# Moved fills, a fold among the first maxima, and layer 1's shift through a small transpose: a two-layer transformer kernel

## The chip, the cores and the metric

The kernel runs on one core of a Trainium2 chip. The metric is device time in microseconds of one launch. The kernel before took 1236.22 us (median of three runs, 1233.09 to 1239.17). One more execution was taken under the profiler; its rows are the durations quoted here.

## The reference, cut to what matters

Two transformer layers over 2048 tokens of 128 channels, all in float32. Each layer is: modulation (a 128-vector through a sigmoid-linear unit and a 128x768 matrix gives six vectors: shift, scale and gate, twice), a layer norm, attention, a gated residual, a second norm, a feed-forward part and a gated residual.

```python
mod = (_silu(L0_c) @ L0_wmod).reshape(...)      # sa, ca, ga, sb, cb, gb
ga = (2 * (ga >= 0) - 1) * jnp.maximum(jnp.abs(ga), 0.25)     # gb alike
h = _layernorm(x) * (1 + ca) + sa
x = x + ga * _L0_attn_ref(h, ...)   # 16 heads of 8, softmax over all 2048 keys
h = _layernorm(x) * (1 + cb) + sb
x = x + gb * _L0_ffn_ref(h, ...)    # 16 experts, one per token, and a shared one
...
x = x + ga * _L1_attn_ref(h, ...)   # 8 query heads of 16, one key head, causal
x = x + gb * _L1_ffn_ref(h, ...)    # mixes each token with the one before it
```

## The kernel before, in words

**Engines.** A planner takes the program as written and gives each engine its own order: an instruction is placed when the planner thinks its inputs ready, the earliest written first. `tc.keep_in_program_order(ins)` pins an instruction behind the one written before it on its engine. On the chip each engine then runs its list strictly in that order.

**Start.** `first_norm` takes the four blocks of 512 tokens: statistics on DVE, square root (L648) on ACT, reciprocal and normal on DVE, four transposes on PE, and the eviction into `hT` on ACT (L237). `modulation(0)` runs between.

**Stacks.** A product of two float32 numbers is made from two reduced-precision halves each, hi and lo. Keys and queries are split (`split`, L239), and their halves are stacked in four interleaved row sets by DMAs (`stack`, L256), so that one pass over 64 rows per head gives the whole product. Layer 0 has 8 stacks (`kS0`), two heads each. Every eighth row set ends in a row of ones for the shift: `fill(st)` (L669) writes a whole stack [128 x 2048] from `last_rows`, a column with ones at rows 31, 63, 95 and 127, before the DMAs write the other rows. Fills 0 and 1 are written ahead of `first_norm`; fills 2 to 7 in `begin0`, each ahead of its stack's DMAs. All eight are on ACT. Stacks 0 and 1 go out on SP and ACT, the others on SP alone.

**Attention** (L287) runs units (block b of 512 queries, group of four heads): 16 units in layer 0 and 8 in layer 1. `first_pass(u)` makes the scores [128 queries x 1024] and takes their maxima on DVE (L385, or L390 with the causal mask). `largest` (L394) negates them and splits each into two halves in `nm`. `turn` (L411) transposes `nm` so that the negated maxima, called the shift, become rows. `second_pass(u)` makes the scores the other way round (L458), exponentiates them on ACT (L468) and multiplies them with the values on PE (L484). The first pass runs eight steps (`LEAD`) ahead of the second. Three score banks in PSUM are shared by both passes; two more serve the values and everything else (`other_bank`).

In layer 0 (`fused`) the turn is one transpose of 32 columns, a copy and eight DMAs on SP (L424), which put the rows into the query stack. In layer 1 `nm` is [128 x 4 x 128] with the maxima at the first columns of each 64; four transposes give `mT` with the rows in place, and two extra products (L464) add them. A turn is called two or three steps after its unit's last maximum (`turns`, L438 and L591). `turn` is written after `project_q(b + 1)` in layer 1 for the units with the first group of a block: `project_q` (L348) is put into `ready` while unit 2b's first pass runs, and ends in 16 DMAs on SP into a query stack that two blocks share.

**Fold.** `fold0` (L810) makes layer 1's modulation and gates, spreads a gate over the weights of the shared expert (GpSimd, L815) and folds the first gate into the output weights of attention. It is the first of the `late` pieces, which are taken during unit 0's second pass.

Of the kernel before, what the change touches and what calls it, by code (L numbers as in the profile page):

```python
# [10 lines left out]
F32 = mybir.dt.float32  # L11
# [8 lines left out]
P = 128  # L20
T = 2048
# [22 lines left out]
def two_layers(ctx: ExitStack, tc: tile.TileContext, a: dict, out: bass.AP):  # L44
# [48 lines left out]

    last_rows = const.tile([P, 1], F32, name="last_rows")
    nc.vector.tensor_reduce(last_rows, ident[:, 31::32], AX.X, ALU.add)


    mods = []  # L100
    sg = const.tile([P, 2], F32, name="sg")
    sc = const.tile([P, 2], F32, name="sc")

    def modulation(layer, ps):
        if layer == 0:
            nc.scalar.activation(sg, vcol(V_C0, 2), AF.Sigmoid)
            nc.vector.tensor_mul(sc, sg, vcol(V_C0, 2))
        for j in range(6):
            nc.tensor.matmul(ps[:, j:j + 1], wmod[layer][:, j * P:(j + 1) * P],
                             sc[:, layer:layer + 1], start=True, stop=True)  # L110
# [25 lines left out]
    for i, at in enumerate((ident.rearrange("p (r c) -> p r c", c=4)[:, :, 2:4],  # L136
# [24 lines left out]
    nc.gpsimd.affine_select(out=ones_f, in_=ones_f, compare_op=ALU.is_gt, fill=0.0,  # L161
                            base=0, pattern=[[1, P]], channel_multiplier=-1)
    before_r = const.tile([P, P], F32R, name="before_r")
    nc.scalar.copy(before_r, ones_f)

    rank = const.tile([P, NE], F32, name="rank")
    for e in range(NE):
# [119 lines left out]
    def attention(layer, hT, ngrp, dk, scale, causal, kvp, begin, prepare, wq, bq, folded, ended,  # L287
# [23 lines left out]
        with ExitStack() as s:  # L311
# [26 lines left out]
            negmax = []  # L338
            for i in range(2):
                shape = [P, nst, TB, S, 2] if fused else [P, TB, P]  # L340
                t = kvp.tile(shape, F32, name=f"{L}nm{i}", tag=f"nm{i}")
                nc.gpsimd.memset(t, 0.0)
                negmax.append(t)

            units = [(b, grp) for b in range(NB) for grp in range(ngrp)]
            attended = {}
# [1 line left out]
            def project_q(b):  # L348
                if b in qS:
                    return  # L350
                ps = other_bank()
                nc.tensor.matmul(ps, wq, hT[:, b * QB:(b + 1) * QB], start=True, stop=True)
# [13 lines left out]
                qS[b] = t  # L366

            def first_pass(u):
# [5 lines left out]
                def step(i, kb, pair):  # L374
                    own = causal and kb == b
                    n = (i + 1) * P if own else QB
                    ps = ps_s.tile([P, 2, QB], F32, name=f"{L}p1_{u}_{i}_{kb}_{pair}", tag="s")
                    for j in range(2):
                        g = 2 * pair + j
                        st, r = grp * nst + g // S, RT * (g % S)  # L380
                        nc.tensor.matmul(ps[:, j, :n], qS[b][r:r + RT, st, i * P:(i + 1) * P],  # L381
                                         kS(st)[r:r + RT, kb * QB:kb * QB + n],
                                         start=True, stop=True)
                    if not own:
                        nc.vector.tensor_reduce(pm[:, i, 2 * pair:2 * pair + 2, kb], ps,  # L385
                                                AX.X, ALU.max)
                    for j in range(2 if own else 0):

                        g = 2 * pair + j
                        nc.vector.tensor_tensor_reduce(  # L390
                            masked[:, :n], ps[:, j, :n], later[:, QB - n:], 1.0, LOWEST,
                            ALU.add, ALU.max, pm[:, i, g, kb:kb + 1])

                def largest():  # L394
# [3 lines left out]
                    if fused:  # L398


                        parts = [(nm[:, k],
                                  nx[:, :, k * S:(k + 1) * S]) for k in range(nst)]
                    else:

                        parts = [(nm.rearrange("p t (g w) -> p t g w", w=RT)[:, :, :, 2 * k:],
                                  nx[:, :, k * S:(k + 1) * S]) for k in range(nst)]
                    for v, nk in parts:
                        nc.vector.tensor_copy(v[:, :, :, 0].bitcast(F32R), nk)
# [2 lines left out]
                def turn():  # L411
                    nm = negmax[u % 2]
                    ps = other_bank()
                    if fused:
                        n = nst * TB * 2 * S
                        mT = qp.tile([n, P], F32R, name=f"{L}mT{u}", tag="mT")
                        nc.tensor.transpose(ps[:n, :P], nm.rearrange("p k t g w -> p (k t g w)"),  # L417
                                            ident)
                        nc.scalar.copy(mT, ps[:n, :P])  # L419

                        for k in reversed(range(nst)):
                            for i in range(TB):
                                r = (k * TB + i) * 2 * S
                                nc.sync.dma_start(  # L424
                                    out=qS[b][31::32, grp * nst + k,
                                              i * P:(i + 1) * P].bitcast(F32),
                                    in_=mT[r:r + 2 * S, :].bitcast(F32))
                    else:
                        mT = qp.tile([P, QB], F32R, name=f"{L}mT{u}", tag="mT")
                        for i in range(TB):  # L430
                            nc.tensor.transpose(ps[:, i * P:(i + 1) * P], nm[:, i, :], ident)
                        nc.scalar.copy(mT, ps)
                    shift[u] = mT

                steps = [(lambda i=i, kb=kb, pair=pair: step(i, kb, pair))
                         for i in range(TB) for kb in range(nkb) for pair in range(HG // 2)]
                last = steps.pop()
                return steps + [lambda: (last(), largest(), turns.append([0, turn]))]  # L438

            def second_pass(u):  # L440

# [114 lines left out]


            shift, late, turns, weights, ready = {}, [], [], [], []
            if not folded:
                late.append(lambda: folded.extend(fold0(other_bank())))  # L560

            def all_first():
                for u in range(len(units)):
# [3 lines left out]
                    for i, step in enumerate(first_pass(u)):  # L567
# [66 lines left out]
    def first_norm():  # L634

        with tc.tile_pool(name="ln0", bufs=2) as wp, \
# [3 lines left out]
            def start(b):  # L640
# [25 lines left out]
    pool = a0.enter_context(tc.tile_pool(name="a0kv", bufs=1))  # L666
    kS0 = pool.tile([P, H0 * RT // P, T], F32R, name="kS0", tag="kS")

    def fill(st):  # L669

        nc.scalar.activation(kS0[:, st, :], last_rows.to_broadcast([P, T]), AF.Copy)

    for st in range(2):
        fill(st)
# [3 lines left out]
    def begin0(ep, pp, stacks):  # L678
# [14 lines left out]
        for pair in range(NB // 2):  # L693
# [5 lines left out]
            cols = slice(pair * 2 * QB, (pair + 1) * 2 * QB)  # L699
            split(ps.rearrange("p j n -> p (j n)"), vcol(V_BK), hi[:, cols], lo[:, cols])  # L700

        for st in range(nst):
            rows = slice(st * 2 * D0, (st + 1) * 2 * D0)
            queues = (nc.sync, nc.scalar) if st < 2 else (nc.sync,)
            if st >= 2:
                fill(st)
            stack(kS[:, st, :], (hi[rows], lo[rows]), (0, 1, 0, 1), queues, RT // D0)
            stack(stacks[0][:, st, :], (qhi[rows], qlo[rows]), (0, 0, 1, 1), queues, RT // D0)
        for b in range(NB):
            for pair in range(TB // 2):  # L710
                ps = pp.tile([P, 2, QB], F32, name=f"pv{b}{pair}", tag="s")
                for j in range(2):
# [94 lines left out]

    gb = const.tile([P, P], F32, name="gb")

    def fold0(bank):  # L810
        modulation(1, bank)
        gates(1)
        nc.tensor.matmul(bank[:, :P], m[:, 5:6].to_broadcast([P, P]), ident, start=True, stop=True)
        nc.scalar.copy(gb, bank[:, :P])
        nc.gpsimd.tensor_tensor(wsd, wsd, gb.unsqueeze(1).to_broadcast([P, NS, P]), ALU.mult)  # L815
        wog, rows = fold_gate(pool, bank, wo0, vcol(V_BO), m[:, 2:3], "a0")
        for b in range(NB):
            add_rows(b, rows)
        return [wog]

    folded1 = []

# [546 lines left out]
```

## Time and profile before

The profiled execution took 1246.91 us, of which the span from the first to the last instruction is 1245.2 us. The mean granted clock of the tensor engine was 0.942.

| engine | busy us | share of the span | instructions |
|---|---|---|---|
| PE (matmul) | 1146.1 | 92% | 9216 |
| PEld (weight load) | 519.8 | 42% | 9216 |
| DVE | 953.1 | 77% | 1550 |
| ACT | 766.6 | 62% | 845 |
| POOL | 85.0 | 7% | 152 |

How to read it: a share of busy time is a mean over the whole span. The parts that the change touches lie in the first 100 us (start and unit 0) and in the stretch from 920 to 1220 us (layer 1's attention), so they have to be looked at there. "SPq" and "ACTq" are the queues of the two engines that issue DMAs; an issue of about half a microsecond occupies the queue, and the landing comes later. In rows of the timeline, the first number is the start from the span's beginning, the second the length, and a bracket at the end tells how long the engine had been idle and what released it.

### The profile page before, as it was taken

What the parts mean: (1) busy time and instruction counts of PE and PEld (TensorE: products, weight loads), DVE (VectorE), ACT (ScalarE), POOL (GpSimd) and SP (SyncE); (2) the same over time, 40 slices, a digit from 0 to 9 for tenths busy, and PEclk for the clock granted to TensorE, in tenths of its full rate; (3) what the DMA queues carried; (4) which work ended last, traced back from release to release, by engine and by line L of the source; (5) the groups of instructions that cost most, each with busy time, mean ns of one, the idle gap of its engine ahead of it and who ended that gap; (6) DMA issues with size and microseconds to landing.
All of it is one profiled execution on the core that took longest, in us unless ns stands there. A gap on an engine that the chain in (4) does not pass through costs nothing.

```text
span 1245.2 us, 22565 instructions
## 1 busy us (share of the span) xinstructions
PE 1146.1 (92%) x9216; PEld 519.8 (42%) x9216; DVE 953.1 (77%) x1550; ACT 766.6 (62%) x845; POOL 85.0 (7%) x152
## 2 busy tenths in 40 slices
PE   4579999999999999999999999979858999999995
PEld 2233333334433443343343343447624444444443
DVE  4788898899889889889989883343458688898532
ACT  6107777777777777777777778643323355556763
POOL 2002000000000000000000000320321011100101
PEclk9658999999999999999999999999967789999997
DMA  4841010212220212110000000033210101000000
GB/s 125 113 50 35 2 51 3 70 28 77 70 70 2 69 39 79 56 53 2 1 2 2 2 2 2 20 118 91 64 30 15 35 1 35 1 1 1 2 22 13
DMA packets 63880, 45.23 MB, mean 36 GB/s; under 512 B 7009, under 2 KB 57825, under 8 KB 63265
## 3 DMA queue, kind: packets, MB, share of 16 engines
q1 hardware_dynamic: 61008, 40.37, 13.2%
q10 hardware_dynamic: 1744, 1.32, 0.6%
q0 software_dynamic: 1024, 2.10, 0.6%
q8 instruction: 73, 1.20, 0.4%
q14 instruction: 31, 0.25, 0.1%
HBM read 9.88 MB, written 21.95 MB: 26 GB/s over the span
## 4 chain that ended last, share of the span: by engine, by line
PE 80%; DVE 12%; ACT 4%; DMA 1%; issue 1%; another core or an unknown queue 1%; DVEq 0%; SPq 0%; ACTq 0%; POOLq 0%; POOL 0%
PE a0bank L484 24%; PE a0p L458 17%; PE a0p L381 13%; PE a1bank L484 5%; PE a1p L458 4%; DVE a0mx L385 3%; DVE a1mx L385 3%; PE a1p L381 2%; PE a1p L464 2%; DVE a1masked L390 2%; PE sg L987 2%; ACT a0e L468 1%; PE gu L1039 1%; PE a0bank L522 1%
## 5 line engine op out<-in xcount | busy, mean ns | idle before, releaser
L385 DVE TENSOR_REDUCE a0mx<-a0p 128x2 f32<-128x1024 f32 x512 | 623.9, 1225 | 71.3 <-PE a0p L381 61.4
L468 ACT ACTIVATE a0e<-a0p 128x1024 f32<-128x1024 f32 x512 | 521.8, 1024 | 178.7 <-PE a0p L458 154.1
L484 PE MATMUL a0bank<-a0e,vA 128*32 128x256 f32 x4096 | 333.2, 391 | 1.7 <-ACT a0e L468 1.7
L381 PE MATMUL a0p<-kS,a0qS 64*128 64x512 f32 x1024 | 248.2, 480 | 26.4 <-DVE a0mx L385 13.1
L458 PE MATMUL a0p<-a0qS,kS 64*128 64x512 f32 x1024 | 260.5, 497 | 0.0
L468 ACT ACTIVATE a1e<-a1p 128x1024 f32<-128x1024 f32 (+3 forms) x160 | 143.1, 896 | 109.8 <-PE a1p L464 106.6
L458 PEld LDWEIGHTS a0p<-a0qS,kS 64*128 64x128 f32 x1024 | 97.2, 184 | 204.4 <-issue 132.2
L381 PEld LDWEIGHTS a0p<-kS,a0qS 64*128 64x128 f32 x1024 | 100.2, 192 | 111.4 <-ACT a0e L468 57.1
L484 PEld LDWEIGHTS a0bank<-a0e,vA 128*32 128x32 f32 x4096 | 86.3, 108 | 137.8 <-issue 121.5
L385 DVE TENSOR_REDUCE a1mx<-a1p 128x2 f32<-128x1024 f32 x96 | 115.8, 1221 | 14.5 <-PE a1p L381 13.7
L484 PE MATMUL a1bank<-a1e,vA 128*32 128x256 f32 (+1 forms) x1152 | 97.1, 386 | 0.4 <-POOL a1e L471 0.4
L458 PE MATMUL a1p<-a1qS,kS 64*128 64x512 f32 (+3 forms) x320 | 77.7, 470 | 5.2 <-DVE a1mx L385 3.9
L381 PE MATMUL a1p<-kS,a1qS 64*128 64x512 f32 (+3 forms) x320 | 68.2, 426 | 11.4 <-DVE a1mx L390 5.1
L390 DVE CUSTOM_DVE_ANT_0 a1masked<-a1p,later 128x128 f32<-128x128 f32 (+3 forms) x128 | 62.4, 488 | 10.6 <-PE a1p L381 5.2
L793 POOL DMA_INDIRECT sent<-hs,row_i x16 | 16.0, 999 | 707.6 <-DVE ln11xn L229 684.0
L464 PE MATMUL a1p<-a1mT,a1ones 64*128 64x512 f32 (+3 forms) x320 | 62.5, 379 | 0.0
L458 PEld LDWEIGHTS a1p<-a1qS,kS 64*128 64x128 f32 x320 | 32.0, 191 | 63.8 <-issue 25.5
L381 PEld LDWEIGHTS a1p<-kS,a1qS 64*128 64x128 f32 x320 | 33.1, 201 | 38.5 <-DVE a1mx L390 12.7
L484 PEld LDWEIGHTS a1bank<-a1e,vA 128*32 128x32 f32 x1152 | 25.7, 109 | 42.6 <-issue 35.3
L471 POOL TENSOR_SCALAR_AFFINE_SELECT a1e<-a1e 128x256 f32<-128x256 f32 x64 | 26.0, 407 | 234.7 <-ACT a1e L468 234.7
L464 PEld LDWEIGHTS a1p<-a1mT,a1ones 64*128 64x128 f32 x320 | 32.5, 195 | 1.7 <-issue 1.3
L419 ACT CAST a0mT<-a0bank 32x128 fp32r<-32x128 f32 x16 | 4.0, 253 | 41.2 <-PE a0bank L417 41.2
(384 smaller groups left out, 698.7 us busy)
## 6 DMA issues: line engine op xcount, KB each, us to landing
sent<-blank SPq DMA_DIRECT2D x68, 256.0 KB
kS<-a0qS SPq DMA_DIRECT2D x28, 128.0 KB
a0qS<-a0mT SPq DMA_DIRECT2D x128, 2.0 KB
wgu_sb<-in_gate_up SPq DMA_DIRECT2D x1, 2048.0 KB
a0qS<-a0qh SPq DMA_DIRECT2D x62, 32.0 KB
a0qS<-a0ql SPq DMA_DIRECT2D x62, 32.0 KB
xs<-sent SPq DMA_DIRECT2D x31, 64.0 KB
y_rows<-y SPq DMA_DIRECT2D x7, 256.0 KB
```

Source lines behind the costliest of these rows:

```text
L381: nc.tensor.matmul(ps[:, j, :n], qS[b][r:r + RT, st, i * P:(i + 1) * P], kS(st)[r:r + RT, kb * QB:kb * QB + n], start=True, stop=True)
L385: nc.vector.tensor_reduce(pm[:, i, 2 * pair:2 * pair + 2, kb], ps, AX.X, ALU.max)
L390: nc.vector.tensor_tensor_reduce(masked[:, :n], ps[:, j, :n], later[:, QB - n:], 1.0, LOWEST, ALU.add, ALU.max, pm[:, i, g, kb:kb + 1])
L458: nc.tensor.matmul(ps[:, j, q0:], kS(st)[r:r + RT, kt * P:(kt + 1) * P], qS[b][r:r + RT, st, q0:], start=True, stop=fused)
L464: nc.tensor.matmul(ps[:, j, q0:], ones[r:r + RT, g // S, :], shift[u][r:r + RT, q0:], start=False, stop=True)
L468: nc.scalar.activation(e[:, :, q0:], ps[:, :, q0:], AF.Exp, scale=scale)
L471: nc.gpsimd.affine_select(out=e[:, :, q0:q0 + P], in_=e[:, :, q0:q0 + P], compare_op=ALU.is_ge, fill=0.0, base=0, pattern=[[0, 2], [1, P]] ...
L484: nc.tensor.matmul(av[g * W:(g + 1) * W, c0:c1], vA(kt, grp * HG + g), held[kt, g // 2][:, g % 2, c0:c1], start=(kt == 0 and c0 == 0), sto ...
L522: nc.tensor.transpose(ps[:, i * P:(i + 1) * P], o[:, i * P:(i + 1) * P], ident)
L793: nc.gpsimd.indirect_dma_start(out=sent[t], in_=hs[:, i, :], in_offset=None, out_offset=bass.IndirectOffsetOnAxis(ap=row_i.bitcast(U32)[:, ...
L987: nc.tensor.matmul(ps[:, j, :], w[:, k * P:(k + 1) * P], hT[:, b * QB:(b + 1) * QB], start=True, stop=True)
L1039: nc.tensor.matmul(ps[:, i, :], xsT[q][:, i * P:(i + 1) * P], wgu[:, bass.ds(regs[j], 1), :].rearrange("p a f -> p (a f)"), start=True, st ...
```

## The change

In the start, `last_rows` gets a second column. The first is now summed on GpSimd, and the first square root is pinned behind fills 0 and 1 on ACT. Fills 2 to 7 are made by GpSimd from the second column, which DVE copies, pinned behind the last split of the keys. A second tile, `before_f`, takes the masked ones, so that `ones_f` is not written over. A small exp at the end of `begin0` loads its table there.

In unit 0's first pass, `fold0` becomes three pieces that are taken after steps 5, 11 and 17, with the modulation's products pinned. The maxima of the first eight steps of unit 1 are pinned, so is `project_q(1)`'s product, and the turn of unit 0 is called two steps sooner.

In layer 1 unit 0 keeps the four transposes (of a tile `wide`). Units 1 to 7 take one transpose of 32 columns, a copy, and eight DMAs on SP into `rows_of`, two tiles whose other rows are zero.

```diff
-    last_rows = const.tile([P, 1], F32, name="last_rows")
-    nc.vector.tensor_reduce(last_rows, ident[:, 31::32], AX.X, ALU.add)
+    last_rows = const.tile([P, 2], F32, name="last_rows")
+    first = last_rows[:, 0:1]
+    nc.gpsimd.tensor_tensor(first, ident[:, 31:32], ident[:, 63:64], ALU.add)
+    for i in (95, 127):
+        nc.gpsimd.tensor_tensor(first, first, ident[:, i:i + 1], ALU.add)
...
+                rows_of = [kvp.tile([P, QB], F32R, name=f"{L}rows{i}") for i in range(2)]
+                nc.gpsimd.memset(rows_of[1].bitcast(F32), 0.0)
...
+                if fused and b == 1:
+                    tc.keep_in_program_order(product)
...
+                        if fused and u == 1 and i == 0:
+                            tc.keep_in_program_order(found)
...
-                    if fused:
-                        n = nst * TB * 2 * S
-                        mT = qp.tile([n, P], F32R, name=f"{L}mT{u}", tag="mT")
...
+                    n = nst * TB * 2 * S
+                    if fused or u:
+                        small = qp.tile([n, P], F32R, name=f"{L}mT{u}", tag="mT")
+                        nc.tensor.transpose(
+                            ps[:n, :P], nm.rearrange("p a t b w -> p (a t b w)"), ident)
+                        nc.scalar.copy(small, ps[:n, :P])
+                        for c in reversed(range(nst if fused else S)):
                             for i in range(TB):
...
+                                if fused:
+                                    dst = qS[b][31::32, grp * nst + c, cols]
+                                else:
+                                    dst = rows_of[u % 2][c * RT:c * RT + 4, cols]
+                                nc.sync.dma_start(out=dst.bitcast(F32),
+                                                  in_=small[r:r + 4, :].bitcast(F32))
...
-                return steps + [lambda: (last(), largest(), turns.append([0, turn]))]
+                return steps + [lambda: (last(), largest(),
+                                         turns.append([2 if fused and u == 0 else 0, turn]))]
...
-            if not folded:
-                late.append(lambda: folded.extend(fold0(other_bank())))
+            folds = [] if folded else fold0(other_bank, folded)
...
                         step()
+                        if folds and i % 6 == 5:
+                            folds.pop(0)()
...
-                nc.scalar.activation(rstd, mv[:, :, 1], AF.Sqrt, bias=eps)
+                root = nc.scalar.activation(rstd, mv[:, :, 1], AF.Sqrt, bias=eps)
+                if b == 0:
+                    tc.keep_in_program_order(root)
...
-    def fill(st):
-
-        nc.scalar.activation(kS0[:, st, :], last_rows.to_broadcast([P, T]), AF.Copy)
+    def fill(st, i=0):
+
+        dst, src = kS0[:, st, :], last_rows[:, i:i + 1].to_broadcast([P, T])
+        if i == 0:
+            nc.scalar.activation(dst, src, AF.Copy)
+        else:
+            nc.gpsimd.tensor_copy(dst, src)
...
+        tc.keep_in_program_order(nc.vector.tensor_copy(last_rows[:, 1:2], last_rows[:, 0:1]))
+        for st in range(2, nst):
+            fill(st, 1)
...
-            if st >= 2:
-                fill(st)
...
+        t = lnp.tile([P, TB], F32, name="exptable", tag="y")
+        nc.scalar.activation(t[:, :1], vA[:, NT - 1, :1], AF.Exp, scale=0.0)
...
+    def fold0(bank, folded):
+        def second():
+            modulation(1, bank(), tc.keep_in_program_order)
+            gates(1)
+        def first():
+            ps = bank()
...
+        def fold():
+            wog, rows = fold_gate(pool, bank(), wo0, vcol(V_BO), m[:, 2:3], "a0")
+            for b in range(NB):
+                add_rows(b, rows)
+            folded.append(wog)
+        return [second, first, fold]
```

More of the change, by code (lines that the diff above doesn't have):

```diff
@@ L102, in two_layers, with modulation @@
     sc = const.tile([P, 2], F32, name="sc")
-    def modulation(layer, ps):
+    def modulation(layer, ps, place=lambda ins: ins):
         if layer == 0:
@@ L108, in modulation @@
         for j in range(6):
-            nc.tensor.matmul(ps[:, j:j + 1], wmod[layer][:, j * P:(j + 1) * P],
-                             sc[:, layer:layer + 1], start=True, stop=True)
+            place(nc.tensor.matmul(ps[:, j:j + 1], wmod[layer][:, j * P:(j + 1) * P],
+                                   sc[:, layer:layer + 1], start=True, stop=True))
         m = const.tile([P, 6], F32, name=f"mod{layer}", tag=f"mod{layer}")
@@ L160, in two_layers @@
     nc.scalar.copy(ones_r, ones_f)
-    nc.gpsimd.affine_select(out=ones_f, in_=ones_f, compare_op=ALU.is_gt, fill=0.0,
+    before_f = const.tile([P, P], F32, name="before_f")
+    nc.gpsimd.affine_select(out=before_f, in_=ones_f, compare_op=ALU.is_gt, fill=0.0,
                             base=0, pattern=[[1, P]], channel_multiplier=-1)
     before_r = const.tile([P, P], F32R, name="before_r")
-    nc.scalar.copy(before_r, ones_f)
+    nc.scalar.copy(before_r, before_f)
     rank = const.tile([P, NE], F32, name="rank")
@@ L337, in attention @@
             masked = kvp.tile([P, QB], F32, name=L + "masked") if causal else None
[L338 to L343, printed above, removed]
+            negmax = [kvp.tile([P, nst, TB, S, 2] if fused else [P, S, TB, nst, 2], F32,
+                               name=f"{L}nm{i}", tag=f"nm{i}") for i in range(2)]
+            if not fused:
+                wide = kvp.tile([P, TB, P], F32, name=L + "wide")
+                nc.gpsimd.memset(wide, 0.0)
+                rows_of = [kvp.tile([P, QB], F32R, name=f"{L}rows{i}") for i in range(2)]
+                nc.gpsimd.memset(rows_of[1].bitcast(F32), 0.0)
             units = [(b, grp) for b in range(NB) for grp in range(ngrp)]
@@ L351, in project_q @@
                 ps = other_bank()
-                nc.tensor.matmul(ps, wq, hT[:, b * QB:(b + 1) * QB], start=True, stop=True)
+                product = nc.tensor.matmul(ps, wq, hT[:, b * QB:(b + 1) * QB], start=True,
+                                           stop=True)
+                if fused and b == 1:
+                    tc.keep_in_program_order(product)
                 hi = kvp.tile([P, QB], F32R, name=f"{L}qh{b}", tag="qh")
@@ L384, in step @@
                     if not own:
-                        nc.vector.tensor_reduce(pm[:, i, 2 * pair:2 * pair + 2, kb], ps,
-                                                AX.X, ALU.max)
+                        found = nc.vector.tensor_reduce(pm[:, i, 2 * pair:2 * pair + 2, kb], ps,
+                                                        AX.X, ALU.max)
+                        if fused and u == 1 and i == 0:
+                            tc.keep_in_program_order(found)
                     for j in range(2 if own else 0):
@@ L402, in largest @@
                                   nx[:, :, k * S:(k + 1) * S]) for k in range(nst)]
+                    elif u:
+                        parts = [(nm[:, :, :, k].rearrange("p g t w -> p t g w"),
+                                  nx[:, :, k * S:(k + 1) * S]) for k in range(nst)]
                     else:
-                        parts = [(nm.rearrange("p t (g w) -> p t g w", w=RT)[:, :, :, 2 * k:],
+                        parts = [(wide.rearrange("p t (g w) -> p t g w", w=RT)[:, :, :, 2 * k:],
                                   nx[:, :, k * S:(k + 1) * S]) for k in range(nst)]
@@ L413, in turn @@
                     ps = other_bank()
-                    if fused:
-                        n = nst * TB * 2 * S
-                        mT = qp.tile([n, P], F32R, name=f"{L}mT{u}", tag="mT")
[L417 to L421, printed above, removed]
-                            for i in range(TB):
[L423 to L427, printed above, removed]
+                    n = nst * TB * 2 * S
[5 more added lines that the diff above has]
+                        for c in reversed(range(nst if fused else S)):
+                            for i in range(TB):
+                                cols = slice(i * P, (i + 1) * P)
+                                r = (c * TB + i) * 4
+                                if fused:
[4 more added lines that the diff above has]
+                                                  in_=small[r:r + 4, :].bitcast(F32))
                     else:
-                        mT = qp.tile([P, QB], F32R, name=f"{L}mT{u}", tag="mT")
                         for i in range(TB):
-                            nc.tensor.transpose(ps[:, i * P:(i + 1) * P], nm[:, i, :], ident)
-                        nc.scalar.copy(mT, ps)
+                            nc.tensor.transpose(ps[:, i * P:(i + 1) * P], wide[:, i, :], ident)
+                        nc.scalar.copy(rows_of[0], ps)
+                    mT = None if fused else rows_of[u % 2]
                     shift[u] = mT
@@ L808, in two_layers @@
     gb = const.tile([P, P], F32, name="gb")
[L810 to L819, printed above, removed]
+    def fold0(bank, folded):
[4 more added lines that the diff above has]
+            ps = bank()
+            nc.tensor.matmul(ps[:, :P], m[:, 5:6].to_broadcast([P, P]), ident, start=True,
+                             stop=True)
+            nc.scalar.copy(gb, ps[:, :P])
+            nc.gpsimd.tensor_tensor(wsd, wsd, gb.unsqueeze(1).to_broadcast([P, NS, P]), ALU.mult)
+        def fold():
[4 more added lines that the diff above has]
+        return [second, first, fold]
     folded1 = []
```

## The prediction

> **What bounds the kernel now.** I read the page's slices first, then the chain of waits over the first 160 us, then tables by stretch, then the timeline at the places that the change touches.
>
> The slices (31 us each):
>
> ```profile
> PE   4579999999999999999999999979858999999995
> DVE  4788898899889889889989883343458688898532
> PEclk9658999999999999999999999999967789999997
> ```
>
> From slice 4 to slice 26 PE is full at nearly the whole clock: layer 0's attention is bound by PE. Slices 0 to 3 are not, and that is where the first half of the change works. Layer 1 (from slice 29) is bound by PE again, with DVE close behind: from 1020 to 1070 us PE is busy 47.8 of 50 us and DVE 44.8.
>
> The chain of waits at the start (start, length, what):
>
> ```profile
> 19.36 1.80 ACT kS L671
> 21.16 0.67 ACT hT L237
> 21.82 1.80 ACT kS L671
> 23.62 0.67 ACT hT L237
> ...
> 39.43 3.75 DMA kS<-a0qS
> 43.18 0.79 PE a0p L381 x2
> 44.00 36.30 DVE a0mx L385 x32
> ```
>
> Three things in it: fills of kS (L671) alternate with the hT evictions on ACT; then the stacking DMAs hold everything until 43.1; then DVE's 32 maxima of unit 0 run back to back. The table by stretch (length, then busy PE, PEld, DVE, ACT, POOL with counts, clock, DMA share, GB/s) shows what limits each:
>
> ```profile
> 44.00:80.20 36.20, 25.44 (x66) 9.00 (x64) 36.20 (x32) 0.00 (x0) 0.00 (x0) 0.50 0.80 92
> 80.20:98.20 18.00, 12.74 (x41) 7.51 (x41) 13.00 (x31) 5.34 (x8) 5.77 (x5) 0.50 0.00 1
> ```
>
> In the first DVE has no gap, 36.20/32 = 1.13 us a step, while PE has 0.34 us idle a step. In the second nobody is full: 18 us in which DVE does 10 maxima (11.3 us) and waits 5. The timeline there:
>
> ```profile
> 84.32 4.59 SPq L424 DMA_DIRECT2D a0qS<-a0mT  x8
> 84.65 2.72 PE L109 MATMUL a0bank<-sc,wmod_sb 128*128 128x1 f32 x12
> 88.14 2.36 DVE L385 TENSOR_REDUCE a0mx<-a0p 128x2 f32<-128x1024 f32 x2 [1.76 <-PE a0p L381]
> 92.92 0.79 PE L458 MATMUL a0p<-a0qS,kS 64*128 64x512 f32 x2
> ```
>
> PE does layer 1's modulation just where unit 0's second pass should start, and DVE runs dry.
>
> **Part A, fills and roots (0 to 43 us).** Fills 0 and 1 ran at 13.55 to 17.45 on ACT because last_rows came from DVE at 13.47. With three GpSimd adds after ident (ready at 1.82) they fit from 3.57, when ACT has issued its DMAs. ACT then has two fills of 1.90, two table loads of 1.28 and the sigmoid's 0.20 before the first root: 3.57 + 6.56 = 10.1, against 8.17 before. Its reader, the reciprocal, ran at 11.89, behind DVE's wait for the modulation, so this is free; if Copy needs a table load of its own it is 11.4, still free. The evictions then follow their transposes. DVE's own order sets them: its work between 10.9 and 16.1 stays, then two reciprocals and two normals (2 x 1.25) bring the last xn to about 18.6, and hT3 to 19.8 instead of 24.29: 4.5 us earlier. Project_q(1)'s product (1.92 us of PE at 20.07) leaves this place too. Next, the split of pk waited for the fill at 26.55 to 28.45, some 1.0 us, which goes: the last lo ends at about 26.9 instead of 32.27. Gain at this point 5.4.
>
> The fills of stacks 2 to 7 go to GpSimd behind that lo. No row has one of 128x2048. Nearest: the cast of 128x256 at 0.394, eight times 3.15; by the slope of the 128x4096 memset (3.50) 1.9. I take 2.0: six fills from 27 to 39 (to 46 at the dear end). They are read by DMAs for units 1 to 3, and unit 1's maxima start near 73: hidden. GpSimd beside DVE: the maxima during L285's adds (93.7 to 98.6) took 1.22 to 1.28 as elsewhere, so I count nothing.
>
> The landing that PE waited for at 43.0 was a 32 KB piece of ql issued on ACT at 37.22, stuck behind the 128 KB pieces of stacks 0 and 1 and of later stacks that SP had put into the same engines. Stacks 0 and 1 are 8 x 128 KB and 16 x 32 KB, about 1.3 MB to the last piece. Between 30 and 46 the DMAs moved 131 GB/s. If later stacks do not mix in (they wait for a fill until 29 at least), the last lands near 34.5, a gain of 8.6; if they do as now, the gain is the 5.4 above. I take 7.0.
>
> **Part B, fold and turn (43 to 98 us).** Among unit 0's maxima the fold costs DVE its small operations: some 16 at 0.07 and the 0.29 of wog, 1.3. Its 12 pinned products hold PE 2.7 us. DVE has at most two filled banks, 2.3 us, and PE needs 0.79 for the next: about 1.2 lost. Two or four products of 0.2 to 0.3 later fit into the slack. A DVE wait for the products at the low clock, as at 10.91 (2.35), could add 2. Sum 2.5 to 4.5; I take 3.
>
> After unit 0 the maxima of unit 1 are pinned behind the negated maxima, so nm is ready 0.6 after the 32nd maximum, not 2.8 (L409 ended at 82.98). Eight DMAs of 2 KB: SP is 4.59 us issuing them, first packets 1.2 after the first issue, last at 89.5, 5.3 after the cast. The shift lands about 0.6 + 0.7 + 5.3 = 6.6 after the 32nd maximum; the eight steps ahead need 9.0. The score gets its bank after the sixth (7.3), and exp follows at 8.7. Before it was 95.52 - 80.21 = 15.3. Gain 15.3 - 8.7 - 3 = 3.6. Exp's table load (94.22, 1.28) is inside this. The Trainium skill (ScalarE: Activation LUTs, "What ACT_TABLE_LOAD costs") prices a switch at 2.66 with its drain; here exp started at 95.52, right behind the 1.28, so the row decides; by the page B would gain 1.4 more. Project_q(1)'s product now lies in PE-bound work: minus 1.0. **B gains 2.6**, between 0.5 and 5.
>
> **Part C, layer 1's shift.** Units 1 to 7 save PE three of four transposes: four take 0.66 in the chain, one 0.26 (L417): 7 x 0.39 = 2.7, and PE is the bound. ACT's cast falls from 0.58 to 0.25. But the rows then go through eight DMAs on SP. The rows of unit 4 (the cast, the first product that reads it, and the DMAs of project_q(3)):
>
> ```profile
> 1044.74 0.58 ACT L432 CAST a1mT<-a1bank 128x512 fp32r<-128x512 f32 x1 [2.18 <-PE a1bank L431]
> 1045.76 1.11 SPq L260 DMA_DIRECT2D a1qS<-a1qh  x2
> 1046.70 0.39 PE L464 MATMUL a1p<-a1mT,a1ones 64*128 64x512 f32 x2
> ```
>
> From the start of the cast to its first reader there are 1.96 us here. In units 1 to 7, by the same rows: 3.96, 6.62, 11.29, 1.96, 7.75, 3.30, 5.65. The new way needs, from the old start of the cast, -0.3 (fewer transposes) + 0.25 + 5.3 + 0.1 = 5.4. Late: unit 1 by 1.4, unit 4 by 3.4, unit 6 by 2.1; 6.9 in all. PE is in order, so L381 for the next maxima stands behind the waiting L464, and DVE lives on two banks, 2.3 us. The skill (DMA: Bandwidth & Descriptors, "Anatomy of one DMA") gives a small DMA a fixed cost of about 2.0 us, mostly the receipt: by it only unit 4 is late, by 0.1, and C is a gain of 2.6. This trace shows eight issues of 0.57 in line, so the row decides. How much of 6.9 is covered is unknown: nothing (the wait sits in PE's queue) to all of it (products of the first pass and of L484 placed ahead of the score). I take half, 3.5. **C costs 0.8**, between -2.7 and +4.2.
>
> **Sum.** -7.0 - 2.6 + 0.8 = -8.8 against the profiled execution (1246.91; span 1245.2 and 1.7 around it), about 1238. It ran 10.7 above the median of the runs, 1236.22; I take the same difference off that: **1227.5**. Bounds: -8.6 - 5 - 2.7 = 1220; -5.4 - 0.5 + 4.2 = 1234.5.
>
> **Rivals.**
> 1. The shift's wait is not covered at all: 6.9 instead of 3.5, so 1231. For it: DVE is nearly full at unit 4, so a dry DVE is lost. Against: L484 and L381 stand near each boundary and could be put first.
> 2. SP's order, the slower side. Project_q(b+1) is written before the turn of unit 2b, and its 16 DMAs wait in SP's queue for the last scores of the block that owned the buffer:
>
> ```profile
> SPq L260 <- PE a1p L458: 97.7, 2, 51.1
> ```
>
> If they stand ahead of the turn's eight at unit 4, these start at 1056 (16 at 0.65 from 1045.76), land at 1061, 14.8 late instead of 3.4; with 2 covered that is 11 more: 1239. If at unit 2 as well (issues from 983.6 to 994.6, needed at 985.9, 14 late): 1251. It decides as soon as the 16 come first. For it: at unit 4 the cast ends only 0.8 before those DMAs are free. Against: at unit 2 that margin is 4 us.
> 3. The front gains less: the DMAs land as late as now after the split, and DVE waits for the fold: -5.4 - 0.5 + 0.8, so 1231.
>
> **Chances.** Forecast 0.57, rival 1 0.13, rival 2 0.18, rival 3 0.12. The range for eight in ten is 1220 to 1239: it takes in the bounds and the one-boundary case of rival 2. Half a per cent, about what a measurement here can tell from no change, is 6.2 us, so faster means below 1230. The forecast gives most of it, the rivals 1 and 3 mostly "same", rival 2 slower in two of three: faster 0.52, same 0.30, slower 0.18.
>
> **What would show it.** Right: the last hT eviction near 20; the second score product near 36 instead of 43.1; the first exp near 85 instead of 95.5; L464's wait for a DMA at units 1, 4 and 6, each under 3.5 us. Wrong: a start of the maxima after 40; a DVE gap over 3 us at the modulation; any L464 that waits over 5 us, with project_q's DMAs ahead of the turn's on SP.

## The result, and the profile after

The changed kernel took 1244.94 us (median of nine runs, 1242.19 to 1252.92), against 1238.63 us of the kernel before on the same chip (nine runs, 1233.09 to 1240.67). The ratio of the means is 1.0072, interval 1.0046 to 1.0098: slower by 0.7%, some 9 us (6.3 between the medians). In a later session, on another chip, the same two kernels gave 1257.75 and 1246.45 us, ratio 1.0087 (1.0074 to 1.0100). The forecast was 1227.5.

The profiled execution of the changed kernel took 1244.0 us (span 1241.2), 3 us less than that of the kernel before. This comparison misleads. The chain of waits of the kernel before has this piece, in the experts' stage, which the change doesn't touch:

```profile
900.84 9.88 another core or an unknown queue
```

PE, DVE and ACT all stand still for 6.9 us of it. The same stop, of 9.67 to 9.89 us, is in every profile of the two sessions in which the kernel before took 1246 to 1247 us. It is in no profile of a changed or tried kernel from the sessions in which the kernel before took 1236 to 1239 us, the first profile of the changed kernel among them. Its cause is not known, but it is of the size by which the profile before, which has it, ran above its runs (10.7 us). So the profiles have to be read stage by stage, and totals compared only within one session.

The slices of the changed kernel, as before 31 us each:

```profile
PE   5669999999999999999999999979878996999995
DVE  5798898889889889889899982353487896897532
PEclk9559999999999999999999999999976997998997
```

Slices 0 to 2 are still not full (slice 3 was nearly full before, too, though the prediction counts it with them). The start, in the timeline of PE (start, length, engine, line, operands, count, and in brackets how long PE was idle and for what):

```profile
20.73 2.07 PE L713 MATMUL pq<-hT,wq_sb 128*128 128x512 f32 x2 [0.87 <-ACT hT L241]
22.60 4.50 PE L721 MATMUL pk<-hT,wk_sb 128*128 128x512 f32 x8
...
35.95 0.80 PE L390 MATMUL a0p<-kS,a0qS 64*128 64x512 f32 x2 [3.60 <-DMA kS<-a0qS]
39.31 1.65 PE L390 MATMUL a0p<-kS,a0qS 64*128 64x512 f32 x6 [2.57 <-DMA kS<-a0qS]
```

The last hT eviction ends at 20.68, near the 19.8 forecast. But pq takes 2.07 us for the two products that took 1.12 before, pk 4.50 for 3.60. In two stretches, counting only what writes or reads pk (length, then busy PE, PEld, DVE, ACT with counts, clock, DMA share, GB/s), a step shows:

```profile
22.60:24.30 1.70, 1.70 (x2) 0.67 (x2) 0.00 (x0) 0.00 (x0) 1.00 0.00 0
24.79:26.94 2.15, 2.15 (x6) 0.76 (x4) 0.37 (x1) 1.11 (x1) 1.00 0.44 90
```

The first two products fill 1.70 us; the last five fill 2.15 (the sixth in the count is the end of the one before), half the time each, 0.43 us. The clock column is no help here: the profile has no record of the clock ahead of the step to full speed at 24.41 us, and 1.00 is printed in its absence. In the kernel before that record begins at 22.58, ahead of pq, so that pq and pk ran fast there from the first product.

The second score product starts at 39.31. The chain tells what it waited for:

```profile
32.64 6.47 DMA kS<-a0qS
39.12 0.20 issue
39.31 0.81 PE a0p L390 x2
40.15 2.37 DVE a0mx L394 x2
```

The second maximum, from which DVE runs almost without gaps, starts at 40.15 instead of 44.00: 3.85 us earlier. (In the second profile of the same kernel, experiment 3, it starts at 42.44; the step of the clock came at 28.11 there. So places in the start vary by some 2 us from one profile to the next.) Then by stretch (length, busy PE, PEld, DVE, ACT, POOL with counts, clock, DMA share, GB/s):

```profile
42.40:78.20 35.80, 27.16 (x78) 12.64 (x78) 35.07 (x48) 0.53 (x2) 8.86 (x6) 0.50 0.77 87
78.20:88.50 10.30, 5.96 (x17) 2.14 (x17) 10.28 (x13) 1.28 (x2) 0.86 (x1) 0.50 0.01 2
88.50:100.00 11.50, 11.50 (x66) 4.14 (x67) 7.60 (x7) 6.45 (x7) 0.00 (x0) 0.67 0.04 9
```

DVE has no gap in the second stretch any more, where it had 5 us; in the third PE is full, but at two thirds of its clock. The first exp starts at 87.05 instead of 95.52, 8.5 us earlier, but the eleventh at 105.14 instead of 109.68, and the last of layer 0 at 806.43 instead of 812.57: the front is worth 4 to 6 us of the 9.6 forecast. The granted clock goes from 0.50 to 1.00 at 96.1 us here and at 101.1 in the kernel before, so only 5 us of the exps' lead were kept by the clock.

Layer 1 gives more than that back. SP's queue at unit 4, then PE:

```profile
1024.57 2.59 SPq L442 DMA_DIRECT2D a1rows<-a1mT  x4
1027.26 1.14 SPq L264 DMA_DIRECT2D a1qS<-a1qh  x2
...
1036.08 1.23 SPq L264 DMA_DIRECT2D a1qS<-a1ql  x2
1037.36 2.52 SPq L442 DMA_DIRECT2D a1rows<-a1mT  x4
```

```profile
1032.37 0.94 PE L560 MATMUL a1bank<-a1wog,a1onT 128*128 128x128 f32 x6
1041.05 1.85 PE L481 MATMUL a1p<-a1rows,a1ones 64*128 64x512 f32 x6 [7.75 <-DMA a1rows<-a1mT]
```

Four of the turn's eight DMAs (L442) stand ahead of project_q(3)'s 16 (L264), the other four behind them. The shift's product starts 16.8 us after the cast (1024.29), and PE stands for 7.75 us. At units 1, 6 and 7 it waits for the same DMAs by 1.58, 1.71 and 1.10 us.

### The profile page after: what moved, and what is told of

Its sections match the earlier page's. It is cut to its first block, busy times and chain, and to the rows that moved or that the text cites. A ratio compares the mean times of both kernels' runs of the same rounds, so it can differ in the third digit from the quotient of the medians.

```text
span 1241.2 us, 22639 instructions
## 1 busy us (share of the span) xinstructions
PE 1149.3 (93%) x9195; PEld 520.0 (42%) x9195; DVE 955.8 (77%) x1550; ACT 754.7 (61%) x840; POOL 96.3 (8%) x159
## 4 chain that ended last, share of the span: by engine, by line
PE 81%; DVE 10%; ACT 3%; DMA 2%; SPq 1%; issue 1%; ACTq 0%; DVEq 0%; POOL 0%; POOLq 0%
PE a0bank L501 24%; PE a0p L475 18%; PE a0p L390 13%; PE a1bank L501 5%; PE a1p L475 4%; DVE a0mx L394 3%; PE a1p L390 3%; PE a1p L481 3%; PE sg L1024 2%; DVE a1masked L401 2%; DVE a1mx L394 1%; ACT a0e L485 1%; PE gu L1076 1%; ACT a1e L485 1%; PE a0bank L539 1%
## 5 line engine op out<-in xcount | busy, mean ns | idle before, releaser
L390 PEld LDWEIGHTS a0p<-kS,a0qS 64*128 64x128 f32 x1024 | 100.2, 192 | 106.9 <-ACT a0e L485 58.0
L390 PE MATMUL a1p<-kS,a1qS 64*128 64x512 f32 (+3 forms) x320 | 72.2, 434 | 8.9 <-DVE a1mx L401 4.5
L481 PE MATMUL a1p<-a1rows,a1ones 64*128 64x512 f32 (+3 forms) x320 | 65.5, 396 | 12.1 <-DMA a1rows<-a1mT 12.1
L481 PEld LDWEIGHTS a1p<-a1rows,a1ones 64*128 64x128 f32 x320 | 34.8, 203 | 14.7 <-issue 14.2
L998 ACT ACTIVATE sigs<-sg 128x512 f32<-128x512 f32 x12 | 7.2, 598 | 24.8 <-PE sg L1024 24.8
```

Of the source, the lines that this page charges most:

```text
L481: nc.tensor.matmul(ps[:, j, q0:], ones[r:r + RT, g // S, :], shift[u][r:r + RT, q0:], start=False, stop=True)
```

## The experiments

Ratios are to the kernel before, measured in the same session. There were four: experiments 1 to 4; 6 to 8; 5 with the repeats marked "again"; and 9. Places in a profile are compared across sessions only where the text says so, and differences there of less than some 2 us decide nothing.

**1. The front alone.** Layer 1's turn is the old one, with its layout of `nm`; the line that decides:

```diff
-                    if fused or u:
+                    if fused:
```

> The changed kernel with layer 1's old shift (four transposes of 128 columns, no DMA), so parts A and B alone. In the changed kernel's profile unit 0's second maximum came 3.85 us earlier than before and the last exp of layer 0 6.1 us earlier. Theory 1 (the front gains, layer 1's shift loses): 4 to 6 us under the kernel before, ratio 0.995 to 0.997, and from the start of layer 1 on the same intervals as before. Rival (the front's gain is lost again in the experts' stage or in layer 1, whatever turns the shift): ratio 1.000 or above.

Measured: 1241.63 against 1247.04 us, ratio 0.9961 (0.9949 to 0.9973): 4.9 us faster by the ratio. In its profile the second maximum starts at 39.71 and the last exp of layer 0 5.0 us earlier than before. The front's gain is kept; it is half of what I forecast.

**2. Layer 1's turn alone.** The kernel before with `wide`, `rows_of` and the one transpose, and nothing else.

> The kernel before with layer 1's new shift (one transpose of 32 columns, eight DMAs) and nothing else, so part C alone. Theory 1 (SP's order at unit 4: four of the turn's eight DMAs stand behind project_q's 16): 9 to 12 us over the kernel before, ratio 1.007 to 1.010, with a wait of 7 us or more of the shift's product for a DMA at unit 4 and short ones elsewhere. Theory 2 (each of the seven units is late by the eight DMAs' own latency): about the same total, but spread, 1 to 3 us at each of units 1, 4, 6 and 7. My prediction's term: +0.8, ratio 1.001.

Measured: 1263.46 against 1247.04 us, ratio 1.0144 (1.0118 to 1.0169), 16 us slower between the medians and 18 by the ratio: more than either theory said. The waits of PE (total, times, longest):

```profile
PE a1p L471 <- DMA a1rows<-a1mT: 11.4, 4, 7.7
```

One wait of 7.7, as theory 1 had it, and three short ones: 11.4 us of standing still. The loss is larger, although PE is spared transposes. The stretch of layer 1's attention (first to last exp) in the kernel before and in this one shows where the rest lies:

```profile
938.11:1220.75 282.64, 268.80 (x2264) 129.26 (x2266) 210.15 (x511) 157.24 (x186) 31.26 (x68) 0.93 0.04 11
939.28:1236.83 297.55, 275.05 (x2243) 130.76 (x2245) 211.19 (x511) 154.68 (x185) 31.38 (x68) 0.90 0.04 11
```

The stretch is 14.9 us longer: PE is idle for 8.7 us more, and busy for 6.2 us more with 21 products fewer, at a clock of 0.90 instead of 0.93. The two parts add up to 1.0105 (1.0144 - 0.0039), where the change gave 1.0072 and 1.0087; within the intervals these agree.

**3. SP's order.** In layer 1 the 16 DMAs of project_q(2) and project_q(3) are held back until the turn has issued its own:

```diff
-                for st in range(P // dk // S):
-                    ...
+                def put(): ...
+                held_back.append(put)
...
+                    while held_back:
+                        held_back.pop(0)()
```

> The changed kernel, but the 16 DMAs of layer 1's project_q(2) and project_q(3) are written behind the turn of their block's first unit, so that all eight of the turn's DMAs come first in SP's queue. Theory 1 (SP's order): unit 4's shift lands 10 us earlier, 9 to 12 us under the changed kernel: ratio to the kernel before 0.995 to 0.998. Theory 2 (latency of eight DMAs at every unit): unit 4 gains no more than 3 us, ratio 1.003 to 1.007.

Measured: 1250.32 us, ratio 1.0035 (1.0013 to 1.0057). That is in the range of theory 2, not of theory 1, although unit 4 did what theory 1 said (below). The changed kernel beside it in one session:

> The changed kernel itself, beside the next two on one chip, since the shares of order and number have so far come from different sessions (order by ratio 0.0037, in the profiles 9 us). All theories: 1.005 to 1.010.

> The turn's eight DMAs first in SP's queue, a second time. Theory 1 (order at unit 4 costs what the profiles show): 7 to 11 us under the changed kernel of the same session, ratio lower by 0.006 to 0.009. Rival (order matters little, number does): lower by no more than 0.004.

Measured: 1257.75 us (1.0087) and 1249.58 us (1.0029, 1.0019 to 1.0039), so the order costs 8.2 us, or 0.0058 of the ratio, just short of theory 1's 0.006 and above the rival's 0.004. SP in the second, around unit 4:

```profile
1040.00 5.09 SPq L449 DMA_DIRECT2D a1rows<-a1mT  x8
1045.19 1.14 SPq L264 DMA_DIRECT2D a1qS<-a1qh  x2
```

All eight are ahead now. But the kernel is still slower than before, by 3.6 us, and 8.5 slower than the front alone. PE still waits at the four units; two of them:

```profile
1046.27 1.19 PE L490 MATMUL a1p<-a1rows,a1ones 64*128 64x512 f32 x4 [1.42 <-DMA a1rows<-a1mT]
...
1127.59 0.93 PE L490 MATMUL a1p<-a1rows,a1ones 64*128 64x512 f32 x4 [1.70 <-DMA a1rows<-a1mT]
```

**4. Two DMAs for eight.** On experiment 3's kernel (the repeat: on the changed kernel, with nothing held back), the negated maxima are laid out so that the four windows of a stack leave as one DMA of 8 KB:

```diff
-        parts = [(nm[:, :, :, k].rearrange("p g t w -> p t g w"),
+        parts = [(nm[:, :, 2 * k:2 * k + 2, :, 0].rearrange("p g w t -> p t g w"),
...
-        for i in range(TB):
-            nc.sync.dma_start(out=rows_of[u % 2][c * RT:c * RT + 4, cols], ...)
+        nc.sync.dma_start(out=rows_of[u % 2][c * RT:c * RT + 4, :]..., in_=small[c * 16:(c + 1) * 16, :])
```

> As the run with the turn first, and the eight DMAs of 2 KB are two of 8 KB (the negated maxima are laid out so that four windows of a stack leave as one). Theory 1: what is left of the wait after the order is mended is the issue of eight at 0.57 us each, so two save some 3.4 us at each unit whose shift is late (units 1, 4, 6: up to 5 us in all if nothing covers them): ratio 0.991 to 0.996. Theory 2 (the latency is in the landing, not in the issues): no difference to the run with the turn first, within 1 us.

> The changed kernel with two DMAs of 8 KB for the eight of 2 KB, and project_q's DMAs not held back: SP's order comes out as with them held back. Theory 1: 9 to 13 us under the run with the turn first, 18 to 22 under the changed kernel, ratio to the kernel before 0.990 to 0.994.

Measured: 0.9927 (0.9906 to 0.9949) and 0.9929 (0.9914 to 0.9943); 12.3 us under the run with the turn first, 20.5 under the changed kernel of the session, 9 us **faster than the kernel before**. In the first session the gain over the run with the turn first was 13.5 us; theory 1 had "up to 5", so its ratio came true without its sum. With two DMAs SP's order is right without anything held back:

```profile
1034.86 1.29 SPq L435 DMA_DIRECT2D a1rows<-a1mT  x2
1036.25 1.16 SPq L264 DMA_DIRECT2D a1qS<-a1qh  x2
```

Both are issued in 1.29 us instead of 5.09, and PE waits nowhere for them. The waits for the rows in the run with the turn first come to 5.8 us, half of the gain. By stretch, the whole of layer 1's attention in the changed kernel again, with the turn first, and with two DMAs:

```profile
934.01:1233.55 299.54, 276.67 (x2243) 130.81 (x2245) 211.33 (x511) 154.68 (x186) 31.21 (x68) 0.90 0.04 11
```

```profile
935.48:1223.52 288.04, 271.30 (x2243) 128.15 (x2245) 210.26 (x511) 154.88 (x185) 31.25 (x68) 0.93 0.05 12
```

```profile
931.39:1210.52 279.13, 265.76 (x2243) 125.27 (x2245) 210.04 (x511) 154.91 (x185) 31.30 (x68) 0.95 0.05 12
```

The same 2243 products take 276.7, 271.3 and 265.8 us: the clock falls from 0.95 to 0.93 and 0.90. Between the first two the stretch differs by 11.5 us, more than the 8.2 between the medians; the profiled run of the changed kernel was the slowest of its five. Between the last two the stretch differs by 8.9 us: 3.4 of idle time (16.7 against 13.4) and 5.5 of slow products. The other 3 us or so of the gain lie outside this stretch. In these two profiles 4.1 us lie ahead of it, in stages that the two kernels share; in the first session's pair the stretch gives 9.6, with 0.4 ahead of it and 1.5 behind. They were not traced. Around unit 4's wait, with the turn first:

```profile
1043.00:1046.27 3.27, 1.61 (x9) 0.82 (x9) 2.52 (x4) 0.59 (x1) 0.00 (x0) 1.00 0.01 3
1046.27:1048.00 1.73, 1.73 (x7) 1.00 (x8) 0.08 (x1) 0.87 (x1) 0.00 (x0) 0.65 0.44 111
1048.00:1050.00 2.00, 2.00 (x9) 1.07 (x9) 1.24 (x2) 1.31 (x3) 0.00 (x0) 0.50 0.39 100
1050.00:1052.00 2.00, 2.00 (x16) 0.78 (x16) 1.33 (x7) 1.49 (x2) 0.00 (x0) 0.95 0.40 98
```

and at the same place with two DMAs:

```profile
1039.00:1041.00 2.00, 1.90 (x16) 0.80 (x12) 1.82 (x2) 1.76 (x3) 0.00 (x0) 1.00 0.41 105
1041.00:1043.00 2.00, 1.77 (x13) 0.93 (x16) 1.48 (x6) 1.24 (x3) 0.00 (x0) 1.00 0.40 100
```

In the first, PE is busy for 1.61 of 3.27 us; then, with work enough, it runs at half the clock for 3.4 us, which by estimate (half of that time) costs 1.7 us more. The wait of 1.70 at unit 6 is followed by 3.4 us at 0.50 too. That of 1.10 at unit 7 is not:

```profile
1173.97:1177.40 3.43, 3.43 (x30) 1.58 (x30) 0.29 (x1) 2.28 (x3) 0.00 (x0) 1.00 0.00 0
```

Nor does a wait of one length always do the same: one of 1.46 us for DVE, which is no part of the change, is followed by 3.4 us at 0.50 in the two-DMA kernel (from 1005.2) and by none in experiment 1 (from 1007.7). So a wait can cost twice, and over the stretch the slow products cost more than the idle time; what decides in the single case is not shown. The planner also gives PE another order around unit 4 in the two kernels, so not all of the 8.9 us need be the waits'.

Start of each unit's exps, counted from the first exp of layer 1, and the end of the kernel counted from there, show where the losses stand:

| kernel | unit 1 | unit 2 | unit 4 | unit 6 | unit 7 | end |
|---|---|---|---|---|---|---|
| old turn (experiment 1) | 15.8 | 47.6 | 107.1 | 186.4 | 231.9 | 304.3 |
| changed, again | 18.8 | 47.9 | 122.1 | 201.0 | 248.8 | 324.2 |
| turn first, again | 18.8 | 47.9 | 111.7 | 192.9 | 239.4 | 311.6 |
| two DMAs, again | 15.8 | 46.9 | 106.9 | 185.2 | 230.5 | 303.4 |

Unit 1's loss of 3.0 us is nearly made up by unit 2. Those at units 4 and 6 are not made up.

**5. The turn alone with two DMAs**, on the kernel before:

> The kernel before with layer 1's one transpose and two DMAs, and nothing else: part C with its DMAs mended. Theory 1 (the turn in itself saves PE three transposes in each of seven units, 2.7 us, and its shift is late at no unit): ratio 0.996 to 0.999. Rival (two DMAs are late at units 1, 4 and 6 too, and eat the saving): ratio 0.9995 to 1.003.

Measured: ratio 0.9977 (0.9967 to 0.9988): 2.9 us faster. This is the term "units 1 to 7 save PE three of four transposes", forecast at 2.7; with two DMAs the shift is late at no unit.

**6. The pin on project_q(1) taken away**, on experiment 4's kernel:

```diff
-                if fused and b == 1:
-                    tc.keep_in_program_order(product)
```

> As the run with two DMAs, but project_q(1)'s product in layer 0 is not held in its written place, so that it lies before the first norms' last transposes again, where PE is idle. Theory 1 (PE is cold when pq and pk come, because the product that kept it busy is gone): pk's products follow each other at 0.43 us instead of 0.85, the last lo ends 1.5 to 2 us earlier, the product of 1.6 us leaves the stretch near 95 us: 1 to 4 us under the run with two DMAs, ratio 0.990 to 0.992. Rival (the landing of the stacks' DMAs sets the start whatever PE does): the second maximum within 0.5 us of 39.8, ratio within 0.001 of 0.9927.

Measured: ratio 0.9918 (0.9890 to 0.9947), which doesn't tell the theories apart. PE's timeline says more:

```profile
17.54 2.07 PE L358 MATMUL a0bank<-hT,wq_sb 128*128 128x512 f32 x2
...
21.76 2.08 PE L725 MATMUL pq<-hT,wq_sb 128*128 128x512 f32 x2 [0.87 <-ACT hT L241]
23.63 4.88 PE L733 MATMUL pk<-hT,wk_sb 128*128 128x512 f32 x8
```

The product is back among the transposes, and pq and pk are as slow as without it: my theory 1 falls. The second maximum came at 41.46 us, not within 0.5 of 39.8, so the rival's sign did not come either. The step of the clock to full speed was at 26.19 us here, after three of pk's products; in the profiles of kernels with the old start it came at 22.6 to 23.7, ahead of pq, and in all with the new start at 24.1 to 28.1, within pk. So pq and pk, moved 3 us forward, now stand ahead of a step that did not move with them. What sets its time stays open.

**7. The fold late again**, on experiment 4's kernel: its three pieces are one late piece of unit 0's second pass.

```diff
-            folds = [] if folded else fold0(other_bank, folded)
+            folds = []
+            if not folded:
+                late.append(lambda: [f() for f in fold0(other_bank, folded)])
```

> As the run with two DMAs, but layer 1's modulation and the folds of the gates are taken in one piece ahead of unit 0's second pass, as in the kernel before. Theory 1 (the fold among unit 0's maxima costs DVE 2 us there and saves the second pass's start more): the 32nd maximum 2 us earlier, the first exp 3 to 6 us later, 1 to 4 us over the run with two DMAs, ratio 0.994 to 0.996. Rival (the fold's place is of no account, since the second pass of unit 0 starts with the turn's landing): within 1 us of it, ratio 0.992 to 0.9935.

Measured: ratio 0.9933 (0.9912 to 0.9955), inconclusive. In the profiles the way from the second maximum to the 32nd takes 33.9 us instead of 35.9, and the first exp comes 3.7 us earlier, where I had expected it later; but the modulation then falls among the first exps, the eleventh starts at 108.99 against 103.76, and the last of layer 0 4.4 us later. (Experiment 4's profile is of another session.)

**8. The later fills held back** until stack 1 has landed, on experiment 4's kernel (the edit cut to its new lines):

```diff
+            if st == 2:
+                nc.gpsimd.tensor_scalar(last_rows[:, 1:2], kS[:, 1, T - 1:T].bitcast(F32), 0.0, None, ALU.mult)
+                nc.gpsimd.tensor_tensor(last_rows[:, 1:2], last_rows[:, 1:2], first, ALU.add)
+                for i in range(2, nst):
+                    fill(i, 1)
```

> As the run with two DMAs, but GpSimd's fills of stacks 2 to 7 wait for the landing of stack 1, so that no DMA of a later stack can mix with those of stacks 0 and 1. Theory 1 (the later stacks' 128 KB pieces delay the landing that the first maxima wait for): second maximum at 36 to 38 us instead of 39.8, and up to 3 us less in the whole, ratio 0.990 to 0.993. Rival (stacks 0 and 1 alone take the time: some 1.3 MB at the 130 to 160 GB/s that the front moves): second maximum within 0.5 us of 39.8, or the later stacks come too late for unit 1, which costs up to 5 us.

Measured: ratio 0.9920 (0.9899 to 0.9941). The last landing that the second score product waits for, from its issue, in experiment 4 and here:

```profile
32.77 6.01 DMA kS<-a0qS
```

```profile
33.68 4.63 DMA kS<-a0qS
```

Without later stacks' keys in the DMA engines (some of their query pieces were still issued), the landing takes 1.4 us less. But pk ended 0.9 us later in this profile, with the step of the clock at 26.56 instead of 24.22, and the second maximum comes at 39.34 instead of 39.81. So the later stacks do delay the landing, by some 1.4 us in one profile each. The rival holds for the larger part: 4.6 us are left. In the time of the kernel nothing of it is seen.

**9. PE kept busy during the wait**, on the run with the turn first: the first scores of units 1, 4, 6 and 7 are computed five times, to hold the clock.

```diff
-                    for j in range(2):
+                    again = 5 if not fused and kt == 0 and pair == 1 and u in (1, 4, 6, 7) else 1
+                    for n in range(2 * again):
+                        j, last_n = n % 2, n >= 2 * again - 2
```

> The run with the turn first (eight DMAs, all ahead of project_q's), but at units 1, 4, 6 and 7 PE computes the first scores of the second pass five times instead of once (eight products more each, some 1.6 us at full clock; the last one counts), so that it is busy while the shift is on its way. In the runs with the turn first each wait of 1.1 to 1.7 us was followed by 2 to 4 us at a granted clock of 0.50. Theory 1 (the waits cost twice, once as idle time and again as slow products[...]): with 6.4 us more work on PE the kernel is faster, by 3 to 8 us: ratio 0.9965 to 1.0005 against 1.0029 to 1.0035, and the clock stays at 1.00 through the boundaries. Rival (only the idle time counts, the low clock has another cause): no faster, ratio 1.003 to 1.008. The instruction order around the four places shifts a little with the added products.

Measured: ratio 1.0031 (1.0010 to 1.0051), as without the added work. The number falls to the rival, but the test is void: the planner put the doubled products ahead of others, and PE still waited at units 1, 2, 4 and 6, by 1.71, 2.04, 1.82 and 2.67 us, so PE was not kept busy and the clock was not held. Its expectation also says that each wait was followed by a low clock; at unit 7 none was (experiment 4). That slow stretches come with the waits is seen in the three kernels of experiments 3 and 4; that keeping PE busy would prevent them is not shown.

## Why the prediction was wrong

**The step that failed is "C costs 0.8".** Measured, C is a loss of 16 to 18 us alone (experiment 2), and some 16 beside the front (1.0087 less 0.9961). Its terms:

- *SP's order* was not in the sum; it was rival 2, at a chance of 0.18. Its mechanism and place were right: project_q's DMAs ahead of the turn's at unit 4, not at unit 2, though ahead of four of the eight and not of all. It named 11 us; the runs give 8.2, and unit 4's start moves by 10.4. The argument that should have decided was the one I wrote for it, "at unit 4 the cast ends only 0.8 before those DMAs are free": eight issues of 0.57 us don't fit into a gap of 0.8, and half of them stood behind.
- *The slow clock after the waits* was put at nothing: each wait was charged as idle time only. In the stretch of layer 1's attention the eight DMAs cost 8.9 us against two, 5.5 of it as slow products.
- *"I take half, 3.5"* of the 6.9 us late came near the net idle time, 3.4, but not for its reason. From the start of the cast to the product it took 6.6 to 6.9 us where PE waited, not 5.65; unit 7 was late as well; and PE's waits for the rows come to 5.8.
- *The saving of 2.7* was right (2.9).

Beside its row the prediction set the fixed cost of about 2.0 us from the Trainium skill (DMA: Bandwidth & Descriptors, "Anatomy of one DMA"), by which, as an estimate, C would have been a gain of 2.6. The page states that cost for DMAs that go through GpSimd; these went out on SP, where the eight issues alone took 5.09 us. Letting the row decide was right.

By the prediction's own signs, "any L464 that waits over 5 us, with project_q's DMAs ahead of the turn's on SP" came true.

**A was 2 to 4 us, not 7.0** (the second maximum, 1.6 to 4.3 us earlier in the profiles). "The last lo ends at about 26.9" was 29.57: the last hT came 0.9 later than its step said, and pq and the first of pk ran at half the rate that I took from the rows of before, since the step of the clock did not move forward with them. And 7.0 was the middle of 5.4 and 8.6; the 3.2 between these rested on later stacks delaying the landing, which experiment 8 shows to be worth some 1.4 us.

**B was 0.3 to 2.3 us, not 2.6**: from the second maximum to the end of layer 0 the profile of experiment 1 gains 0.7, and the two of the changed kernel 2.3 and 0.3. "Exp follows at 8.7" was 9.8 after the 32nd maximum, near enough, and the fold cost DVE 1.9 us where I took 3. The "15.3" of the kernel before was counted from 80.21, close to the end of the 33rd maximum (80.30); from the end of the 32nd (79.16) it is 16.4. But half of exp's lead of 8.5 us was gone ten exps later: what comes earlier runs while the clock is still low, project_q(1)'s product (now 1.58 us at 95) with it.

With the measured terms, -4.9 for the front (of another session), -2.9 for the transposes, +12.3 for eight DMAs and +8.2 for their order, the sum is +12.7; the change measured +11.3 in that session. The last two terms are by their making the distance from the changed kernel to that with two DMAs, so the sum tests only that the first two add up: -7.8, where the kernel with two DMAs measured -9.2.

## What to carry to other kernels

When a change replaces engine work by DMAs, count the issues: eight small ones in line on a queue take eight times one, and any that wait behind others' DMAs set the time of all. Where PE stands near full, a wait at a boundary can cost its length and a stretch of slow clock after it: read both, the idle time and the busy time of the same products, stage by stage. If the same bytes can leave in one DMA per block, lay out the source so that they do, before anything else is rearranged.

## What the hardware showed that I had not expected

A PE wait of 1.4 us, in a stretch of 3.3 us in which it was busy for half, was followed by 3.4 us at a granted clock of 0.50. Over the 300 us of the stage the mean fell from 0.95 to 0.90 with the waits of the changed kernel. The Trainium skill (TensorE: Matmul & The Clock Gate, "Why this matters for your kernels") warns of idle gaps of more than about 3 us; here gaps of less than half of that were followed by a slow stretch, though not each time (none after 1.10 us at unit 7, nor after one of 1.46 in experiment 1).

Eight DMAs of 2 KB took SP 5.09 us to issue, two of 8 KB 1.29: for the same 16 KB the number of issues counts (0.64 us each at both sizes).

Which products of the start run fast hangs on when the clock steps up: at 22.6 us in the profile before and at 24.4 in that of the changed kernel, where pq comes 3.6 us earlier and runs slow.
